# Setup of a two-layer graph-attention kernel: score matrix cut into four steps, all of Wv0 in flight at once, biases through products with ones, and two weight matrices sent by another queue

## The chip, the cores and the metric

The kernel runs on one core of a Trainium2 chip. The metric is the device time in microseconds (us), median of several executions. The engines are named as in the profile: PE is TensorE (PEld its weight loads), DVE is VectorE, ACT is ScalarE, POOL is GpSimd, SP is SyncE; a "q" behind a name is that engine's issuing of DMAs.

## The reference, cut to what matters

```python
# x: (128 graphs, 128 nodes, 512), adj: (128, 128, 128), nodemask: (128, 128), all float32
h = maximum(layernorm(x), 0)
# layer 0: attention with a sum per node, then three powers of the transition matrix
Xw = h @ Wv0 + bv0
e  = leaky_relu((Xw @ aw[:512])[:, None, :] + (Xw @ aw[512:])[:, :, None] + ab, 0.2)
T  = adj * exp(e);  T = T / (T.sum(-1, keepdims=True) + 1e-12)
H  = h @ Wk[0] + bk[0] + T @ h @ Wk[1] + bk[1] + T @ T @ h @ Wk[2] + bk[2]
x  = x + relu(H)
h  = maximum(layernorm(x), 0)
# layer 1: scores of one number per node
q, k = split(h @ Wqk);  agg = adj @ (k * mask)
w = mask * (q * agg).sum(-1) / sqrt(512)
x = x + softmax(w)[:, :, None] * (h @ Wv1)
```

The graphs are worked on two at a time, so there are 64 pairs and 64 iterations of a loop. Before the loop the kernel folds weights: Wv0 times aw (so a node's attention term is one dot product), the **score matrix** Wq Wk^T of layer 1 out of Wqk, and sums and differences of weight blocks for a seven-product (Strassen) form of the big products.

## The kernel before: the parts that matter

The setup as it was called, in program order (each engine works its own instructions in this order):

```python
load(0)                      # x and adjacency of pair 0 (SP), adjacency blocks agb (POOL)
...                          # aw copied to all 128 partitions (SP); chunks 0 and 1 of Wqk (ACT)
norm0(0)                     # loads pair 1, normalizes pair 0, sends h out and back by blocks (hd, hv)
attention_weights()          # Wv0 slice by slice in TWO buffers, DVE products with aw, spread; bv0, nm
score_sums(0)
attention(0, ...)            # pair 0's transition matrix t; also transposes agb on DVE
score_matrix()               # all four steps: transposes of Wqk chunks, products
stacked_weights()            # Wk in four blocks by SP; the three rows of bk copied to all partitions
t_transposed(0); begin(0); propagate(0); prepare0(0)
right0.update(combine(...))  # differences of the blocks of Wk
norm0(1); score_sums(1)
...
for p in range(NP + 1): ...  # the loop
```

In each iteration, scores of a pair are spread over all partitions through DRAM by GpSimd, once for layer 0 (`pz`) and once for layer 1 (`pw`):

```python
def spread_pair(col, name, by_dma):
    if by_dma:
        ...
        for j in range(G):
            nc.gpsimd.dma_start(d[j], t[j::S32])                            # pzd / pwd: 4 rows each
        dst = front.tile([P, G, N], FP, name=name, bufs=1)
        nc.gpsimd.dma_start(dst.rearrange("p g n -> p (g n)"), bcast(d, 0, G * N))   # pz / pw: 128 rows
        return dst
```

GpSimd also sends the four block loads `agb` of a pair (256 rows each), so it sends 4 x 256 + 2 x 128 + 4 x 4 = 1296 rows per iteration (a row is one contiguous piece for one partition).

## Time and profile before

| | before |
|---|---|
| median of 3 runs | 2400.05 us (2398.68 to 2400.31) |
| span of the profiled execution | 2394.7 us (its run took 2396.55) |
| TensorE busy | 2338.7 us, 98% |
| idle TensorE before the first wide run | 26.1 us of 57.67 |
| normal iteration | 35.98 us |

I cut traces at four events: the start; the first "wide run" (36 products of t and sx, the first that needs everything of the setup); the first product of layer 1 (e with x); the last aggregate product (h with aT); the end. Busy times by stretch, kernel before (columns: stretch, length, busy us of PE, weight loads, DVE, ACT, POOL with counts, granted clock, DMA share, GB/s):

```profile
0.00:57.67 57.67, 31.54 (x110) 18.96 (x110) 32.89 (x83) 19.32 (x42) 14.45 (x35) 1.00 0.86 231
57.67:100.26 42.59, 38.32 (x178) 33.13 (x178) 28.81 (x77) 7.86 (x16) 1.69 (x3) 1.00 0.32 88
100.26:2359.27 2259.01, 2252.42 (x8589) 1597.95 (x8589) 1754.84 (x4769) 605.19 (x1487) 351.89 (x605) 1.00 0.38 100
2359.27:2394.70 35.43, 16.45 (x35) 6.72 (x33) 14.07 (x33) 3.04 (x12) 1.68 (x3) 0.77 0.17 55
```

Length less PE busy is TensorE's idle time: 26.1, 4.3, 6.6 and 19.0 us. I call the third stretch "the loop" below. One caution on the clock column: it counts the trace's clock records, and time ahead of the first record appears as 1.00. Here the first record is at 33.4 us, and the weight loads just before it were spaced as at half the clock (0.82 us, then 0.43), so the 1.00 of the first stretch is no reading.

### The profile page before, as it was taken

Reading aid. Unit: us, or ns where it says so; the run is one execution under the profiler, and the core shown is the slowest. Engines: PE = TensorE matmul, PEld = TensorE weight load, DVE = VectorE, ACT = ScalarE, POOL = GpSimd, SP = SyncE. Lnnn points to the kernel's source line nnn. Section 1 sums busy time; section 2 is a strip of 40 time slices with the busy share of each in tenths; the row PEclk is TensorE's granted clock in tenths of the full one; section 3 lists DMA queues with packets and bytes.
Section 4 is the critical chain, followed back from the end, with each engine's and each line's share of the span. In section 5 each row is a group of like instructions: output and inputs, shape, how many; then the busy total and the mean of one; then the engine's idle time right before and its main releaser. Section 6 shows DMA issues by size and latency. Waiting matters only on the chain.

```text
span 2394.7 us, 27824 instructions
## 1 busy us (share of the span) xinstructions
PE 2338.7 (98%) x8909; PEld 1656.8 (69%) x8909; DVE 1830.6 (76%) x4958; ACT 635.4 (27%) x1557; POOL 369.7 (15%) x646
## 2 busy tenths in 40 slices
PE   5999999999999999999999999999999999999996
PEld 3676676776776776776776776766766766766763
DVE  5777877877877877878878878778778778778764
ACT  3222222222222222222222223223222222222221
POOL 2011111111111111111111111111111111111100
PEclk9999999999999999999999999999999999999998
DMA  8244343343343343343343343442433443443321
GB/s 227 70 112 112 82 115 102 92 114 103 92 106 105 98 106 103 100 106 100 103 106 100 103 106 86 117 106 82 121 105 81 116 110 83 115 112 82 108 67 49
DMA packets 259300, 245.62 MB, mean 103 GB/s; under 512 B 28560, under 2 KB 184336, under 8 KB 259152
## 3 DMA queue, kind: packets, MB, share of 16 engines
q1 hardware_dynamic: 232624, 216.65, 31.9%
q0 software_dynamic: 22304, 25.09, 5.9%
q10 hardware_dynamic: 4224, 2.10, 0.3%
q8 instruction: 70, 1.15, 0.2%
q14 instruction: 78, 0.64, 0.1%
HBM read 142.93 MB, written 100.79 MB: 102 GB/s over the span
## 4 chain that ended last, share of the span: by engine, by line
PE 86%; DVE 6%; DMA 4%; issue 2%; ACT 1%; POOL 0%; DVEq 0%; SPq 0%; POOLq 0%; ACTq 0%
PE pm L367 72%; PE pt L346 8%; PE pt L442 4%; DMA pwd<-pwt 2%; DMA pw<-pwd 1%; PE pt L334 1%; DVE st L224 1%; PE pm L212 1%; PE pt L330 1%; DVE x L279 1%; DVE x L407 0%; DVE sx L354 0%; DVE sx L353 0%; DVE sx L355 0%; DMA pzd<-pzt 0%
## 5 line engine op out<-in xcount | busy, mean ns | idle before, releaser
L367 PE MATMUL pm<-t,sx 128*128 128x256 f32 x2304 | 507.9, 379 | 1.9 <-DVE sx L354 1.9
L367 PEld LDWEIGHTS pm<-t,sx 128*128 128x128 f32 x2304 | 437.6, 190 | 62.1 <-DVE sx L354 2.7
L367 PE MATMUL pm<-b,x 128*128 128x256 f32 x1536 | 363.0, 379 | 0.0
L367 PE MATMUL pm<-f,sx 128*128 128x512 f32 x768 | 352.9, 595 | 4.8 <-DVE s L421 4.8
L367 PEld LDWEIGHTS pm<-b,x 128*128 128x128 f32 x1536 | 282.2, 190 | 59.6 <-issue 29.7
L290 POOL DMA_DIRECT2D pzd<-pzt x126 | 69.9, 556 | 1443.4 <-DVE pzt L287 1443.2
L367 PEld LDWEIGHTS pm<-f,sx 128*128 128x128 f32 x768 | 145.4, 191 | 191.3 <-issue 159.0
L367 PE MATMUL pm<-e,x 128*128 128x512 f32 x512 | 242.9, 597 | 13.7 <-DVE x L279 13.7
L348 ACT COPY x<-pt 128x512 f32<-128x512 f32 x256 | 147.6, 576 | 356.1 <-PE pt L346 356.1
L346 PE MATMUL pt<-tt,h 128*128 128x256 f32 x1024 | 231.5, 379 | 0.0
L262 DVE SCALAR_TENSOR_TENSOR junk<-h,u_bc 128x512 f32<-128x512 f32 x256 | 177.1, 692 | 64.3 <-ACT h L239 52.9
L346 PEld LDWEIGHTS pt<-tt,h 128*128 128x128 f32 x1024 | 194.5, 190 | 26.9 <-ACT tt L335 0.4
L367 PE MATMUL pm<-b,sx 128*128 128x256 f32 x768 | 176.2, 379 | 0.0
L367 PE MATMUL pm<-t,x 128*128 128x256 f32 x768 | 176.2, 379 | 0.0
L367 PEld LDWEIGHTS pm<-e,x 128*128 128x128 f32 x512 | 97.6, 191 | 110.6 <-issue 90.2
L279 DVE STREAM_TRANSPOSE x<-hv 128x512 f32<-128x512 f32 x256 | 166.3, 687 | 7.5 <-DMA hv<-hd 5.6
L307 ACT ACTIVATE s<-s 128x256 f32<-128x256 f32 x63 | 26.2, 416 | 522.8 <-DVE s L305 522.8
L367 PEld LDWEIGHTS pm<-t,x 128*128 128x128 f32 x768 | 145.9, 190 | 19.8
L367 PEld LDWEIGHTS pm<-b,sx 128*128 128x128 f32 x768 | 145.9, 190 | 19.8
L77 POOL DMA_DIRECT2D agb<-in_adj_dram x256 | 152.9, 602 | 18.1 <-DVE aT L319 7.4
L239 ACT ACTIVATE h<-xg,rs 128x512 f32<-128x512 f32 x128 | 97.2, 806 | 184.2 <-DVE rs L236 184.2
L442 PE MATMUL pt<-h,aT 128*128 128x512 f32 x256 | 130.6, 592 | 0.0
(119 smaller groups left out, 2792.7 us busy)
## 6 DMA issues: line engine op xcount, KB each, us to landing
hd<-h SPq DMA_DIRECT2D x128, 512.0 KB, 3.9
hv<-hd SPq DMA_DIRECT2D x512, 128.0 KB, 5.3
xg<-in_x_dram SPq DMA_DIRECT2D x64, 512.0 KB, 3.6
out_dram<-x SPq DMA_DIRECT2D x64, 512.0 KB, 2.8
ag<-in_adj_dram SPq DMA_DIRECT2D x64, 128.0 KB, 2.9
agb<-in_adj_dram POOLq DMA_DIRECT2D x256, 32.0 KB, 4.5
pz<-pzd POOLq DMA_DIRECT2D x63, 128.0 KB, 5.3
pw<-pwd POOLq DMA_DIRECT2D x63, 128.0 KB, 3.3
```

What stands on the lines that cost most here:

```text
L77: nc.gpsimd.dma_start(agb[p][c * S32:(c + 1) * S32].rearrange("p g q i -> p (g q) i"), v[c])
L212: nc.tensor.matmul(pm[c], wt[0][:, c * P:(c + 1) * P], wt[1], start=(o == 0), stop=(o == DC - 1))
L224: nc.vector.bn_stats(st, src[:, j, :])
L239: nc.scalar.activation(h[:, j, :], src[:, j, :], AF.Relu, bias=rs[:, 1, j:j + 1], scale=rs[:, 0, j:j + 1])
L262: nc.vector.scalar_tensor_tensor(junk, h[:, j, :], 1.0, u_bc[:, a, :], op0=OP.mult, op1=OP.mult, accum_out=s[:, a * G + j:a * G + j + 1])
L279: nc.vector.transpose(dst[:, j].rearrange("p f (n b) -> p f n b", n=Q), hv[:, j].rearrange("p n (f a) -> p f n a", f=Q))
L290: nc.gpsimd.dma_start(d[j], t[j::S32])
L307: nc.scalar.activation(ex, z, AF.Exp)
L346: nc.tensor.matmul(pt[:, c].rearrange("p k n -> p (k n)"), h[:, j, at:at + P], tt[:, j].rearrange("p k n -> p (k n)"), start=True, stop=True)
L348: nc.scalar.copy(X[p][:, 1:3, j, kh].rearrange("p k c n -> p c k n"), pt)
L367: nc.tensor.matmul(bank[:, :r.shape[-1]], left[i][:, k, c * P:(c + 1) * P], r, start=(first and at == 0), stop=(at == len(chunks) - 1), sk ...
L442: nc.tensor.matmul(pa, AT[p][:, j, :], H2[p][:, j, :], start=True, stop=True)
```

## The change

Its intent: start the score matrix as soon as Wqk is there, fill TensorE's waits for pair 0's attention with its four steps, remove the copies of aw, bv0 and bk to all partitions, have all of Wv0 in flight at once, and take the larger part of Wk (W1, W2) off SyncE's line. The core of the diff:

```diff
-    load(0)
+    load_x(0)                                  # agb of pairs 0 and 1 comes later
...
-    nc.sync.dma_start(aw_bc..., bcast(aw, 0, 2 * D))
+    f = [const.tile([P, HC, 2, HD], FP, name=f"f{i}") for i in range(1, 5)]   # room of later weights
+    wv0_sb = [...]                             # four slices of Wv0, aw_bc and a row of aw lie in f
+    ones = const.tile([P, P], FP, name="ones")
...
+    nc.scalar.dma_start(awr, aw.rearrange("n o -> o n"))
+    for c in range(DC):
+        nc.sync.dma_start(wv0_sb[c], wv0[c * P:(c + 1) * P])
...
+    def wv0_sums():
+        for a in range(2):
+            nc.tensor.matmul(pb, ones[0:1, :], awr[:, a * D:(a + 1) * D], start=True, stop=True)
+            nc.scalar.copy(aw_bc[:, a, :], pb)
...
-            nc.vector.scalar_tensor_tensor(junk, bv_bc, 1.0, aw_bc[:, a, :], ...)
+            nc.vector.scalar_tensor_tensor(awc[:, a], awc[:, a], 1.0, bvc, ...)   # 4 columns
+        for a in range(2):
+            nc.tensor.matmul(pc[:, 0:1], ones, ccol[:, a:a + 1], start=(a == 0), stop=(a == 1))
...
     def block0(pool, name, kh, nh):
+        if kh == nh == 0:
+            nc.gpsimd.tensor_copy(t[:, 1, 0, 0:1], wv0_sb[0][:, 0:1])   # gate: after slice 0
         for k in range(1, K):
-            nc.sync.dma_start(t[:, k], src.rearrange("(c p) o -> p c o", p=P))
+            nc.gpsimd.dma_start(t[:, k], src.rearrange("(c p) o -> p c o", p=P))
...
-        PZ[p] = spread_pair(s, "pz", p > 0)
+        PZ[p] = spread_pair(s, "pz", p > 1)    # pair 1 by TensorE
...
     norm0(0)
+    load_x(1)
+    wv0_sums()
+    ...                                        # bvc, awc, ab_bc, bsum, nm: small loads by SP
+    score_matrix(0)
+    stacked_weights()
+    score_matrix(1)
     attention_weights()
+    masks()
     score_sums(0)
+    score_matrix(2)
     attention(0, ...)
-    score_matrix()
-    stacked_weights()
+    score_matrix(3)
+    bias()
```

More of the change, by code (lines that the diff above doesn't have):

```diff
@@ L68, in load, with load_x @@
     def load(p):
+        load_x(p)
+        load_agb(p)
+    def load_x(p):
         s = slice(p * G, (p + 1) * G)
@@ L73, in load, with load_agb @@
         nc.sync.dma_start(ag[p], adj[s].rearrange("b n m -> n b m"))
+    def load_agb(p, gate=None):
+        s = slice(p * G, (p + 1) * G)
         agb[p] = loads.tile([P, G, Q, S32], FP, name="agb", bufs=2)
+        if gate is not None:
+            nc.gpsimd.tensor_copy(agb[p][:, 0, 0, 0:1], gate)
         v = adj[s].rearrange("g (q b) (c i) -> c b (g q) i", b=S32, i=S32)
@@ L86 @@
     ab_bc = setup.tile([P, 1], FP, name="ab_bc")
+    awc = setup.tile([P, 2, DC], FP, name="awc")
+    bvc = setup.tile([P, DC], FP, name="bvc")
     wpool = setup_ctx.enter_context(tc.tile_pool(name="wpool", bufs=2))
-    uctx = ExitStack()
-    upool = uctx.enter_context(tc.tile_pool(name="upool", bufs=2))
-    aw_bc = upool.tile([P, 2, D], FP, name="aw_bc", bufs=1)
-    nc.sync.dma_start(aw_bc.rearrange("p a d -> p (a d)"), bcast(aw, 0, 2 * D))
-    bv_bc = upool.tile([P, D], FP, name="bv_bc", bufs=1)
+    b12 = setup.tile([P, K, HC, HD], FP, name="b12")
+    f = [const.tile([P, HC, 2, HD], FP, name=f"f{i}") for i in range(1, 5)]
+    wv0_sb = [f[c // 2].rearrange("p c k o -> p (c k o)")[:, c % 2 * D:(c % 2 + 1) * D]
+              for c in range(DC)]
+    aw_bc = f[2].rearrange("p c k o -> p (c k o)").rearrange("p (a d) -> p a d", a=2)
+    awr = f[3].rearrange("p c k o -> p (c k o)")[0:1]
     ident = const.tile([P, P], FP, name="ident")
@@ L97 @@
     nc.vector.memset(eps, EPS)
+    ones = const.tile([P, P], FP, name="ones")
+    nc.vector.memset(ones, 1.0)
     def spread(dst, col):
@@ L107, in wqk_chunk @@
         return w
-    wchunks = {o: [wqk_chunk(a, o) for a in range(2)] for o in range(2)}
+    nc.scalar.dma_start(awr, aw.rearrange("n o -> o n"))
+    wchunks = {0: [wqk_chunk(a, 0) for a in range(2)]}
+    for c in range(DC):
+        nc.sync.dma_start(wv0_sb[c], wv0[c * P:(c + 1) * P])
+    wchunks[1] = [wqk_chunk(a, 1) for a in range(2)]
     u_bc = const.tile([P, 2, D], FP, name="u_bc")
@@ L117, with attention_weights @@
     wscale = const.tile([P, B], FP, name="wscale")
-    def attention_weights():
+    def wv0_sums():
+        for a in range(2):
+            pb = ps_t.tile([P, D], FP, name="pt")
+            nc.tensor.matmul(pb, ones[0:1, :], awr[:, a * D:(a + 1) * D], start=True, stop=True)
+            nc.scalar.copy(aw_bc[:, a, :], pb)
         for c in range(DC):
-            w = upool.tile([P, D], FP, name="wv0_sb")
-            nc.sync.dma_start(w, wv0[c * P:(c + 1) * P])
             for a in range(2):
                 junk = front.tile([P, D], FP, name="junk", bufs=1)
-                nc.vector.scalar_tensor_tensor(junk, w, 1.0, aw_bc[:, a, :], op0=OP.mult,
+                nc.vector.scalar_tensor_tensor(junk, wv0_sb[c], 1.0, aw_bc[:, a, :], op0=OP.mult,
                                                op1=OP.mult, accum_out=ucol[:, a, c:c + 1])
-        nc.sync.dma_start(bv_bc, bcast(bv0, 0, D))
-        nc.sync.dma_start(ab_bc, bcast(ab, 0, 1))
-        nc.sync.dma_start(nm, nodemask)
+    def attention_weights():
         for a in range(2):
@@ L135, in attention_weights, with masks @@
         for a in range(2):
-            junk = front.tile([P, D], FP, name="junk", bufs=1)
-            nc.vector.scalar_tensor_tensor(junk, bv_bc, 1.0, aw_bc[:, a, :],
-                                           op0=OP.mult, op1=OP.mult, accum_out=ccol[:, a:a + 1])
-        nc.vector.tensor_scalar(cz, ccol[:, 0:1], ccol[:, 1:2], ab_bc, op0=OP.add, op1=OP.add)
+            nc.vector.scalar_tensor_tensor(awc[:, a], awc[:, a], 1.0, bvc, op0=OP.mult,
+                                           op1=OP.mult, accum_out=ccol[:, a:a + 1])
+        pc = ps_t.tile([P, D], FP, name="pt")
+        for a in range(2):
+            nc.tensor.matmul(pc[:, 0:1], ones, ccol[:, a:a + 1], start=(a == 0), stop=(a == 1))
+        nc.vector.tensor_add(cz, pc[:, 0:1], ab_bc)
+    def masks():
         pm = ps_t.tile([P, DC, P], FP, name="pt")
@@ L154, in block0, with combine @@
     def block0(pool, name, kh, nh):
-        t = pool.tile([P, K, HC, HD], FP, name=name)
+        t = b12 if pool is None else pool.tile([P, K, HC, HD], FP, name=name)
         rows(t[:, 0], wk[0, :, nh * HD:(nh + 1) * HD], kh)
+        if kh == nh == 0:
+            nc.gpsimd.tensor_copy(t[:, 1, 0, 0:1], wv0_sb[0][:, 0:1])
         for k in range(1, K):
             src = wk[k, kh * HD:(kh + 1) * HD, nh * HD:(nh + 1) * HD]
-            nc.sync.dma_start(t[:, k], src.rearrange("(c p) o -> p c o", p=P))
+            nc.gpsimd.dma_start(t[:, k], src.rearrange("(c p) o -> p c o", p=P))
         return t
-    def combine(b11, b12, b21, b22, name, shape):
-        t = [const.tile([P] + shape, FP, name=f"{name}{i}") for i in range(1, 5)]
+    def combine(b11, b12, b21, b22, t):
         nc.vector.tensor_sub(t[0], b12, b11)
@@ L177, in stacked_weights, with bias @@
         blocks0["b11"] = block0(const, "b11", 0, 0)
-        blocks0["b12"] = block0(bpool, "b12", 0, 1)
+        blocks0["b12"] = block0(None, "b12", 0, 1)
         blocks0["b22"] = block0(const, "b22", 1, 1)
         blocks0["b21"] = block0(const, "b21", 1, 0)
-        nc.sync.dma_start(bsum, bcast(bk, 0, D))
-        for k in range(1, K):
-            t = bpool.tile([P, D], FP, name="bk_bc")
-            nc.sync.dma_start(t, bcast(bk, k * D, D))
-            nc.vector.tensor_add(bsum, bsum, t)
+    def bias():
+        pb = ps_t.tile([P, D], FP, name="pt")
+        nc.tensor.matmul(pb, ones[:K, :], bsum[:K], start=True, stop=True)
+        nc.scalar.copy(bsum, pb)
     e = {(kh, nh): e01 if (kh, nh) == (0, 1) else
@@ L190, with score_matrix @@
     right1 = {}
-    def score_matrix():
-        pm = [ps_m.tile([P, D], FP, name="pm") for _ in range(DC)]
-        for o in range(DC):
-            ws = wchunks.pop(o)
-            wt = []
-            for a in range(2):
-                p = ps_t.tile([P, DC, P], FP, name="pt")
-                for c in range(DC):
-                    nc.tensor.transpose(p[:, c, :], ws[a][:, c, :], ident)
-                t = wpool.tile([P, D], FP, name=f"wt{a}")
-                if a:
-                    nc.scalar.copy(t, p.rearrange("p c i -> p (c i)"))
-                else:
-                    nc.scalar.copy(t.rearrange("p (f c a) -> p f c a", f=Q, c=DC),
-                                   p.rearrange("p c (f a) -> p f c a", f=Q))
-                wt.append(t)
-            if o + 2 < DC:
-                wchunks[o + 2] = [wqk_chunk(a, o + 2) for a in range(2)]
-            for c in range(DC):
-                nc.tensor.matmul(pm[c], wt[0][:, c * P:(c + 1) * P], wt[1],
-                                 start=(o == 0), stop=(o == DC - 1))
-        for c in range(DC):
-            for nh in range(2):
-                nc.scalar.copy(e[c // HC, nh][:, c % HC, 0, :], pm[c][:, nh * HD:(nh + 1) * HD])
+    pms = []
+    def score_matrix(o):
+        if o == 0:
+            pms.extend(ps_m.tile([P, D], FP, name="pm") for _ in range(DC))
+        ws = wchunks.pop(o)
+        wt = []
+        for a in range(2):
+            p = ps_t.tile([P, DC, P], FP, name="pt")
+            for c in range(DC):
+                nc.tensor.transpose(p[:, c, :], ws[a][:, c, :], ident)
+            t = wpool.tile([P, D], FP, name=f"wt{a}")
+            if a:
+                nc.scalar.copy(t, p.rearrange("p c i -> p (c i)"))
+            else:
+                nc.scalar.copy(t.rearrange("p (f c a) -> p f c a", f=Q, c=DC),
+                               p.rearrange("p c (f a) -> p f c a", f=Q))
+            wt.append(t)
+        if o + 2 < DC:
+            wchunks[o + 2] = [wqk_chunk(a, o + 2) for a in range(2)]
+        for c in range(DC):
+            nc.tensor.matmul(pms[c], wt[0][:, c * P:(c + 1) * P], wt[1],
+                             start=(o == 0), stop=(o == DC - 1))
+            if o == DC - 1:
+                for nh in range(2):
+                    nc.scalar.copy(e[c // HC, nh][:, c % HC, 0, :], pms[c][:, nh * HD:(nh + 1) * HD])
     def norm_relu(src, name, pool):
@@ L248, in norm0 @@
     def norm0(p):
-        if p + 1 < NP and p + 1 not in xg:
+        if 0 < p < NP - 1:
             load(p + 1)
@@ L316, in attention, with transposed_adj @@
             nc.vector.tensor_scalar(t[:, j, :], ex[:, j, :], d[:, 1, j:j + 1], None, op0=OP.mult)
+        if p > 0:
+            transposed_adj(p)
+    def transposed_adj(p):
         AT[p] = front.tile([P, G, N], FP, name="aT", bufs=3)
@@ L481 @@
     norm0(0)
+    load_x(1)
+    wv0_sums()
+    nc.sync.dma_start(bvc, bv0.rearrange("(p c) -> p c", c=DC))
+    nc.sync.dma_start(awc, aw.rearrange("(a p c) o -> p a (c o)", a=2, c=DC))
+    nc.sync.dma_start(ab_bc, bcast(ab, 0, 1))
+    nc.sync.dma_start(bsum[:K], bk)
+    nc.sync.dma_start(nm, nodemask)
+    score_matrix(0)
+    stacked_weights()
+    score_matrix(1)
     attention_weights()
+    masks()
     score_sums(0)
+    score_matrix(2)
     attention(0, front.tile([P, D], FP, name="junk", bufs=1)[:, :G * N])
-    uctx.close()
-    bpool = setup_ctx.enter_context(tc.tile_pool(name="bpool", bufs=1))
-    score_matrix()
-    stacked_weights()
+    score_matrix(3)
+    bias()
     t_transposed(0)
@@ L492 @@
     prepare0(0)
-    right0.update(combine(name="t", shape=[K, HC, HD], **blocks0))
+    right0.update(combine(t=[const.tile([P, K, HC, HD], FP, name=f"t{i}") for i in range(1, 5)],
+                          **blocks0))
+    load_agb(0, X[0][:, 1, 0, 0, 0, 0:1])
+    load_agb(1)
+    transposed_adj(0)
     norm0(1)
@@ L518 @@
         if p == 0:
-            right1.update(combine(e[0, 0], e[0, 1], e[1, 0], e[1, 1], "f", [HC, 2, HD]))
+            right1.update(combine(e[0, 0], e[0, 1], e[1, 0], e[1, 1], f))
             setup_ctx.close()
```

## The prediction

> **What bounds the kernel now.** I read the page first (engine totals, slices), then the waits of TensorE in three parts of the run, then the busy times of the stretches that these marked off, then the timeline of TensorE and of the queues in the first 60 us. The totals say TensorE:
>
> ```profile
> span 2394.7 us, 27824 instructions
> PE 2338.7 (98%) x8909; PEld 1656.8 (69%) x8909; DVE 1830.6 (76%) x4958; ACT 635.4 (27%) x1557; POOL 369.7 (15%) x646
> ```
>
> Span less busy is 56 us of idle TensorE in the whole run; a change that adds idle nowhere and removes no products can't win more than that. The busy times by stretch (columns: stretch, its length, PE, weight loads, DVE, ACT, POOL, granted clock, DMA share, GB/s) say where the 56 us lie:
>
> ```profile
> 0.00:28.58 28.58, 3.99 (x10) 1.57 (x10) 14.29 (x47) 8.85 (x19) 12.70 (x32) 1.00 0.92 239
> 28.58:57.67 29.09, 27.54 (x101) 17.39 (x101) 18.60 (x36) 10.47 (x23) 1.75 (x3) 1.00 0.81 223
> 57.67:130.00 72.33, 68.06 (x279) 52.32 (x280) 50.92 (x136) 16.54 (x34) 6.90 (x12) 0.98 0.35 92
> 130.00:2320.00 2190.00, 2183.41 (x8356) 1553.48 (x8355) 1713.00 (x4664) 590.34 (x1455) 345.00 (x593) 1.00 0.38 101
> 2320.00:2394.70 74.70, 55.72 (x168) 31.99 (x166) 33.79 (x77) 9.21 (x26) 3.37 (x6) 0.89 0.17 53
> ```
>
> The idle is 24.6 us before 28.58, 1.5 to 57.67 (where the first wide run of layer 0's products with t and sx begins), 4.3 to 130, 6.6 in the whole loop, 19.0 at the end. The diff touches only the setup and the first iteration, so its room is the first 25 us, with the next 1.5. There, the timeline of TensorE (start, length, instruction, idle before it and its releaser) reads:
>
> ```profile
> 16.18 0.45 PE L101 MATMUL pt<-ident,ucol 128*128 128x128 f32 x1 [16.18 <-DVE r L231]
> 25.46 0.48 PE L101 MATMUL pt<-ident,ucol 128*128 128x128 f32 x1 [3.90 <-DVE junk L125]
> ...
> 28.58 0.47 PE L101 MATMUL pt<-ident,col 128*128 128x128 f32 x1 [1.91 <-DVE junk L262]
> 28.84 2.34 PE L201 MATMUL pt<-ident,w 128*128 128x128 f32 x10
> ```
>
> L201 is the first transpose of the score matrix (Wqk). It needs nothing but chunk 0 of Wqk, asked for at 0.8 us, yet stands behind the attention chain: Wv0 product by product, its spread, pair 0's score sums. That chain is late because Wv0 comes in two buffers:
>
> ```profile
> 6.05 0.95 SPq L122 DMA_DIRECT2D wv_sb<-in_L_gnn_Wv_dram  x2
> 16.93 0.33 SPq L122 DMA_DIRECT2D wv_sb<-in_L_gnn_Wv_dram  x1
> 20.86 0.45 SPq L122 DMA_DIRECT2D wv_sb<-in_L_gnn_Wv_dram  x1
> 24.74 0.65 DVE L125 SCALAR_TENSOR_TENSOR junk<-wv_sb,aw_bc 128x512 f32<-128x512 f32 x1
> ```
>
> The fourth slice is asked for at 20.86 and worked on at 24.74. After 28.58 TensorE is the bound: 27.5 of 29.1 us busy. DMA is full meanwhile, 92% at 239 GB/s, so bytes are the second limit of the setup.
>
> **What the Trainium skill says.** "TensorE: Matmul & The Clock Gate", Part 1, says that the array starts at half clock and reaches the full one after about 3.4 us of sustained work, and falls back when idle. The trace before agrees in size: weight loads of the score products start 0.82 us apart at 32.7 to 33.5 and 0.43 us apart from 33.5 on, about 5 us after steady work began; so pieces spread over a gappy stretch can cost double. "DMA: Bandwidth & Descriptors", section "Issuing engines are not separate DMA queues", says that transfers of all issuing engines share the same 16 DMA engines and another issuer saves only issue time. The 92% share over three queues fits. So moving W1/W2 to GpSimd's queue gives no bandwidth; what it can remove is waiting in SyncE's line. "SBUF — State Buffer", in its note on DVE blocking software DMA, warns that descriptors made by GpSimd stall while DVE runs a two-port instruction; the trace before has the small adjacency DMAs on that queue at a steady 0.58 us each beside DVE work, and the DVE work of the setup is of two-input kinds, so I count nothing for it.
>
> **The change part by part.**
> *Bytes.* Gone: the copies of aw to all partitions (0.5 MB), of bv0 (0.25) and of three bk rows (0.75): 1.5 MB, at 239 GB/s 6.3 us of DMA. The adjacency blocks for several pairs, 20 x 32 KB = 0.64 MB in the first 29 us, move behind W0: another 2.7 us. What must land before pair 0's seven products are complete: x and adjacency of pairs 0 and 1 (1.3 MB), Wqk 2.1, Wv0 1.0, h out and back 1.0, Wk 3.1: 8.5 MB, 36 us at 239 GB/s, with 1 us to start about 37; the last block (b21, 0.8 MB) is for the last product alone, so b22 lands near 33. Before, the DVE differences that wait for b22 and b21 started at 40.1 and 43.85.
>
> *Attention chain.* With aT's transpose moved out, the DVE wait of 4.3 us for the adjacency blocks before pair 0's normalization goes, and h comes at about 10 instead of 14. All Wv0 in flight from about 2 us: with x, adjacency and the first half of Wqk that is 2.7 MB, 11 us at 239 GB/s, and some of it later because W1/W2 start as soon as slice 0 is there: about 15. The eight DVE products, 0.69 + 0.08 us = 0.74 each, follow the slices and end near 18 instead of 26.1; spread and copies (2 x 0.59) 20; four score sums of 0.74, 23; pair 0's attention took 31.4 to 34.5, so it ends about 27. Some 8 us earlier. The new bias dot is on 4 columns instead of two products of 0.69: 1 us less of DVE.
>
> *TensorE.* This is the sum that decides. Until 57.67 it did 4.0 + 27.5 = 31.5 us of work; ten lone transposes of 0.45 us are nearer 0.2 when others stand behind them, which leaves about 29. Added: two products with ones for aw (each two instructions of 512 columns, cold 0.85 each: 3.4, though some of it in time that is idle anyway), one for bk (0.9), two narrow ones for cz and two spreads of pair 1 (about 1): 3.5 to 4 us that count. Chunk 0 of Wqk is there at about 8 to 9 us (in the first 29 us such a chunk took a median of 9.4 us to land, under more traffic than now). So even a TensorE that is never idle after that gets to the point of 57.67 at 8.5 + 29 + 4 = 41.5. It will be idle: steps 0 and 1 (each 0.95 transposes + 3.7 products = 4.65 us warm, about 8 cold) fill 8.5 to about 20, then it waits for the spread, for pair 0's score sums, for the copy of each transposed chunk, and for the third and fourth chunk, which are asked for only when steps 0 and 1 have freed their buffers. I take 3 us idle: 44.5. That is 13 us earlier than 57.67.
>
> *Behind it.* The same in count of instructions. Pair 1's spread by TensorE replaces a DMA round of 4 to 8 us, which before was not waited for at 61.5; it is needed because the first products now come sooner. Loads of Wv1, pair 2 and the adjacency blocks of pairs 0 and 1 fall into the first products. I give back 1 us for DVE waiting on one of them. The 3.3 us wait near 100 (its chain is pair 2's score spread through DRAM) is not touched.
>
> Sum: 2400 - 13 + 1 - 1 (less DVE work on the way, bk's additions out of the middle of pair 0's sums) = 2387.
>
> **The rivals.**
> *A: the steps fill everything and the DMA is the bound.* Then pair 0's wide products start when b22 is there and its differences (2 x 1.75 us) done, near 37, and the run is 2380. For: bytes fall, queues no longer block each other. Against: the count above needs 41.5 for TensorE alone unless the cold products with ones vanish in idle time.
> *B: the pieces stay in program order on TensorE.* Then step 2 waits for pair 0's score spread at about 24, so steps 2 and 3 end at 34, transposing t takes 1.5, propagation 3.6, DVE's sums of x 3: about 43 to 45, 2386 to 2388; with half-clock pieces 3 us more, 2391.
> *C: contention.* W1/W2 start right behind the first Wv0 slice, on a third queue; if that queue takes a third of the DMA, Wv0 and Wqk chunks 1 to 3 come 5 us later and both chains stretch: about 2393.
> *D: given back.* In-order DVE waits in the first products for pair 1's h (it goes out behind Wk) or for the late adjacency blocks: up to 5 us, 2391; more would show as idle TensorE between 45 and 60.
>
> **Range and chances.** The room (24.6 + 1.5 us idle, less the 8 us until the first chunk) caps the gain at about 18 to 22 us: below 2378 is unlikely. The low end is A with luck, the high end C and D together: 2378 to 2396. Two per cent is 48 us, more than twice the room, so faster by 2% is next to excluded; slower by 2% would need a new wait in each of 64 iterations, and the diff leaves the loop as it was.
>
> **What would show it.** Right: score transposes start before 10 us; the four Wv0 loads stand together at about 2 us; pair 0's wide run with sx starts at 40 to 47 instead of 57.67; idle TensorE before it about 12 us instead of 26; the loop from there on as long as before to within 3 us. Wrong: TensorE idle for over 4 us between steps 1 and 3; a Wv0 slice landing after 18; DVE waiting for pair 1's h or adjacency between 40 and 60; idle in the loop above 6.6 us, which would mean that the order of the instructions moved there as well.

## The result, and the profile after

| | before | after |
|---|---|---|
| median (6 runs each) | 2400.09 us | 2384.62 us (2381.57 to 2387.23) |
| span of the profiled execution | 2394.7 | 2381.4 |

The ratio is 0.9937, with a 95% interval of 0.9924 to 0.9949. Ratios here are the mean time of one kernel's runs over that of the other's of the same rounds, so not quite the ratio of the medians. The result lies in the range and 2.4 us from the predicted value. But the sum that gave that value was not right in its parts.

The totals and the same four stretches of the changed kernel:

```profile
span 2381.4 us, 27851 instructions
PE 2343.4 (98%) x8921; PEld 1660.8 (70%) x8921; DVE 1828.5 (77%) x4956; ACT 637.7 (27%) x1560; POOL 374.3 (16%) x653
```

```profile
0.00:48.13 48.13, 37.72 (x121) 21.94 (x122) 28.98 (x78) 18.67 (x39) 11.62 (x30) 0.93 0.83 246
48.13:91.49 43.36, 38.55 (x178) 33.05 (x178) 30.23 (x80) 9.83 (x22) 9.07 (x16) 1.00 0.29 81
91.49:2343.88 2252.39, 2249.70 (x8589) 1598.72 (x8589) 1755.25 (x4769) 606.16 (x1487) 351.93 (x605) 1.00 0.38 101
2343.88:2381.40 37.52, 17.45 (x35) 7.05 (x33) 14.07 (x33) 3.04 (x12) 1.68 (x3) 0.75 0.16 51
```

| stretch | before | after | difference |
|---|---|---|---|
| to the first wide run | 57.67 | 48.13 | -9.5 |
| to the first product of layer 1 | 42.59 | 43.36 | +0.8 |
| the loop | 2259.01 | 2252.39 | -6.6 |
| the tail | 35.43 | 37.52 | +2.1 |
| span | 2394.7 | 2381.4 | -13.3 |

These are one execution of each kernel; by the medians the gain is 15.5 us, 2.2 more than the table splits up. So half of the table's gain stands where no line of the diff is: the loop has the same 8589 products before and after, and is 6.6 us shorter; its idle TensorE fell from 6.6 to 2.7 us. And the setup gave 8.8 us rather than 12.

**The setup after.** TensorE's timeline (start, length, line, operation, idle before it and its releaser):

```profile
6.10 1.11 PE L231 MATMUL pt<-ident,w 128*128 128x128 f32 x4
8.85 3.13 PE L231 MATMUL pt<-ident,w 128*128 128x128 f32 x12 [1.63 <-DMA w<-in_L_gnn_Wqk_dram]
11.77 4.83 PE L242 MATMUL pm<-wt,wt 128*128 128x512 f32 x8
17.61 3.70 PE L242 MATMUL pm<-wt,wt 128*128 128x512 f32 x8 [1.01 <-ACT wt L234]
...
27.34 0.47 PE L117 MATMUL pt<-ident,col 128*128 128x128 f32 x1 [2.86 <-DVE junk L292]
...
35.86 3.70 PE L242 MATMUL pm<-wt,wt 128*128 128x512 f32 x8
...
48.13 8.04 PE L402 MATMUL pm<-t,sx 128*128 128x256 f32 x36 [0.72 <-DVE sx L389]
```

The score matrix's transposes now start at 6.10 us, wait once for chunk 0's second half until 8.85, and steps 0 and 1 run early, as intended. But pair 0's score spread (L117 on `col`) is at 27.34, only 1.2 us earlier than the 28.58 of before. DVE shows why:

```profile
7.77 0.69 DVE L148 SCALAR_TENSOR_TENSOR junk<-f,f 128x512 f32<-128x512 f32 x1
...
13.16 1.29 DVE L254 BATCH_NORM_STATS2 st<-xg 128x6 f32<-128x512 f32 x2 [4.69 <-DMA xg<-in_x_dram]
...
19.04 0.17 DVE L159 SCALAR_TENSOR_TENSOR awc<-awc,bvc 128x4 f32<-128x4 f32 x1 [3.99 <-DMA awc<-in_L_gnn_aw_dram]
...
22.89 0.69 DVE L148 SCALAR_TENSOR_TENSOR junk<-f,f 128x512 f32<-128x512 f32 x1
...
33.50 0.48 DVE L346 TENSOR_SCALAR t<-junk,d 128x128 f32<-128x128 f32 x2
```

Between the Wv0 products (L148) DVE has, in its order, the statistics of pair 1's x and the small product for the bias. It stood 4.69 us for x of pair 1 and 3.99 us for a transfer of 4 KB. Wv0 itself had landed before (its four loads were asked for by 3.7 us and took 5.5 us in the median). The last Wv0 product ended at 23.6 instead of the predicted 18, and pair 0's t at 34.0 (before: 34.5) instead of 27. Who was in the way shows in what GpSimd and ScalarE issued:

```profile
6.61 5.93 POOL L190 DMA_DIRECT2D b<-in_L_gnn_Wk_dram  x8
```

```profile
10.68 5.76 ACTq L122 DMA_DIRECT2D w<-in_L_gnn_Wqk_dram  x2
```

The eight loads of W1/W2 (2 MB) went out from 6.6 us on, as soon as Wv0's first slice was there. The small loads behind them took about 10 us to land, and ScalarE stood 5.8 us issuing two loads of Wqk (2.1 us in e8) while finished transposes waited for its copies (the 1.01 at 17.61). Between 10 and 20 us the DMA engines moved 369 GB/s, so it was not that little was moved, but that the wrong bytes came first. The Trainium skill, "DMA: Bandwidth & Descriptors", section "Queues, rings and completion order", says that each DMA engine takes turns between the queue rows that have work; this fits with a third queue taking its share at once, and the 10 us here against 4.0 to 5.2 us in experiment e8 for the same loads is the size of it. The other wait, for pair 1's x, is not explained so: SyncE asked for this x only at 6.46 us, after standing 2.7 us for a load of Wv0, and in e8, with W1/W2 out of the way, DVE still stood 4.36 us for it.

**The clock.** TensorE did 37.72 us of work up to the first wide run. Of these, 4.80 lie ahead of 8.85 us, about where my sum of 33 us begins; 32.9 lie behind it. The stretch's granted clock was 0.93 (with the first clock record at 14.2 us, so not to be compared with the 1.00 of before). By tens of us:

```profile
10.00:20.00 10.00, 8.95 (x22) 4.69 (x23) 2.84 (x13) 1.91 (x4) 2.54 (x4) 1.00 1.07 369
20.00:30.00 10.00, 5.91 (x30) 4.36 (x29) 7.50 (x27) 4.48 (x10) 0.00 (x0) 0.72 0.92 211
30.00:40.00 10.00, 10.00 (x29) 4.91 (x28) 9.01 (x23) 4.66 (x13) 0.00 (x0) 0.93 0.68 207
```

TensorE's gaps in 20 to 30 us (5.9 of 10 busy) go with a clock of 0.72 there; in e8, where the same ten us are 9.3 busy, the trace has no drop. The clock record of the drop is 6.827 us long (24.5 to 31.3) at 0.5, twice 3.413 us, and one at 92.8 us is 3.413 long. The Trainium skill, "TensorE: Matmul & The Clock Gate", Part 1, gives 3413 ns for such a window, so here page and trace agree to the digit.

**The loop.** What shortened it is found in GpSimd's line. Before, in one iteration (711 us) and in the one ahead of it (673 us), the issue of `pw`, with the time that GpSimd stood before it:

```profile
673.15 0.59 POOL L292 DMA_DIRECT2D pw<-pwd  x1 [5.36 <-DMA pwd<-pwt]
711.38 0.59 POOL L292 DMA_DIRECT2D pw<-pwd  x1 [7.60 <-issue]
```

7.60 instead of 5.36, and released by "issue": for about 2 us GpSimd waited for nothing that the profile shows. This pause returns every ten iterations (349, 711, 1072, 1434, 1796, 2157 us). What it does, on DVE and then on TensorE:

```profile
714.97 0.42 DVE L461 TENSOR_REDUCE s<-pw 128x2 f32<-128x256 f32 x1 [1.93 <-DMA pw<-pwd]
```

```profile
729.47 1.98 PE L367 MATMUL pm<-f,sx 128*128 128x512 f32 x4 [0.66 <-DVE s L421]
```

DVE stands 1.93 us for pw, does everything behind it later, and 15 us on TensorE waits for a sum of DVE's. After the change the pause is still there, but it falls somewhere else in the iteration, ahead of a load of adjacency that is not needed for long:

```profile
655.50 0.58 POOL L87 DMA_DIRECT2D agb<-in_adj_dram  x1 [2.20 <-issue]
```

It returns at 1016, 1377, 1738 and 2098 us, always ahead of an agb load. At this point it is a correlation. The experiments e10 and e11 test it.

### The profile page after: what moved, and what is told of

Read it like the earlier page. It is cut to its first block, busy times and chain, and to the rows that moved or that the text cites.

```text
span 2381.4 us, 27851 instructions
## 1 busy us (share of the span) xinstructions
PE 2343.4 (98%) x8921; PEld 1660.8 (70%) x8921; DVE 1828.5 (77%) x4956; ACT 637.7 (27%) x1560; POOL 374.3 (16%) x653
## 4 chain that ended last, share of the span: by engine, by line
PE 90%; DVE 3%; DMA 2%; issue 1%; ACT 0%; POOL 0%; DVEq 0%; POOLq 0%; ACTq 0%
PE pm L402 75%; PE pt L381 8%; PE pt L477 4%; PE pt L369 1%; DMA pwd<-pwt 1%; PE pt L365 1%; DMA pw<-pwd 1%; DVE st L254 0%; DMA pz<-pzd 0%; DVE junk L292 0%; DMA pzd<-pzt 0%; DVE x L309 0%; DVE x L442 0%; DVE x L508 0%; DVE sx L390 0%
## 5 line engine op out<-in xcount | busy, mean ns | idle before, releaser
L402 PE MATMUL pm<-e,x 128*128 128x512 f32 x512 | 243.2, 597 | 13.5 <-DVE x L309 13.5
```

Source lines behind the costliest of these rows:

```text
L402: nc.tensor.matmul(bank[:, :r.shape[-1]], left[i][:, k, c * P:(c + 1) * P], r, start=(first and at == 0), stop=(at == len(chunks) - 1), sk ...
```

## The experiments

They came in three calls of four, each with its own runs of the kernel before on the same chip (medians 2399.31, 2396.05 and 2397.68 us). All gave correct outputs. The theories, as they grew:

1. The front's gain needs the interleaved steps and the earlier data together (e1, e2).
2. W1/W2 start too early; held back, the front is shorter (e3, e8; e12 by another queue).
3. The loop's gain comes of where GpSimd's pause falls (e4, e6, e7 tried to shift it with memsets; e10, e11 with rows). Rival: of something in the front or in the addresses.
4. Addresses modulo 256 bytes matter (formed after e4; e6, e7, e9).

### e1: the four steps alone

```diff
-    def score_matrix():
+    def score_matrix(steps):        # as before, for the given steps
...
     norm0(0)
+    score_matrix((0, 1))
     attention_weights()
     score_sums(0)
+    score_matrix((2,))
     attention(0, ...)
     uctx.close()
     bpool = ...
-    score_matrix()
+    score_matrix((3,))
```

> The kernel before with one part of the change alone: the score matrix in four steps, two of them ahead of pair 0's attention weights, one ahead of its attention, one behind. Wv0 still in two buffers, broadcasts still by DMA, W0 to W2 still on SyncE's queue. Theory 1 (the gain before the first products is TensorE's idle time filled with these steps; nothing else of the change moves the end of pair 0's attention, which stood at 34.5 us before and 34.0 after): the first wide run of products with t and sx starts at 46 to 50 us instead of 57.7, and the run takes 2390 to 2393 us, the loop being as slow as before. Rival (the bytes saved and Wv0 loaded at once are what makes the steps fit): it starts at 53 or later, 2396 or more.

Measured: 2403.43 us, ratio 1.0021 (1.0009 to 1.0033). The first wide run came at 53.94 instead of 57.67, the first product of layer 1 at 100.19 (before 100.26). The steps alone gain nothing: theory 1's numbers (46 to 50, 2390 to 2393 us) failed, the rival's (53 or later, 2396 or more) held. One line of DVE and one of TensorE:

```profile
27.54 1.30 DVE L282 STREAM_TRANSPOSE x<-hv 128x512 f32<-128x512 f32 x2 [5.90 <-DMA hv<-hd]
```

```profile
81.60 10.98 PE L370 MATMUL pm<-t,sx 128*128 128x256 f32 x36 [3.72 <-DVE sx L357]
```

My reading (the wait is measured, its cause argued): starting the steps early frees Wqk's buffers early, so chunks 2 and 3 are asked for among the loads that pair 0's attention needs. DVE stood 5.9 us for hv, and t came at 38.4 instead of 34.5. Then the clock fell, with records at 0.5 at 53.5 and 80.8 us: the 36 products that take 8.04 us at full clock took 9.46 at 53.94 and 10.98 at 81.60.

### e2: everything but the interleaving

```diff
-    score_matrix(0)
     stacked_weights()
-    score_matrix(1)
     ...
-    score_matrix(2)
     attention(0, ...)
-    score_matrix(3)
+    for o in range(DC):
+        score_matrix(o)
     bias()
```

> The changed kernel with all four steps of the score matrix put back behind pair 0's attention; all else as changed. Theory 1: the wide run starts at 54 us or later instead of 48.1, the run takes 2390 to 2394 us. Rival (earlier Wv0 and fewer bytes carry the gain): it stays within 2 us of 48.1 and the run within 2 us of the changed kernel's 2385.

Measured: 2386.83 us, ratio 0.9952 (0.9939 to 0.9965).

```profile
54.92 8.04 PE L402 MATMUL pm<-t,sx 128*128 128x256 f32 x36 [0.72 <-DVE sx L389]
```

First wide run at 54.92 (2.75 earlier than before), first product of layer 1 at 97.15 (3.1 earlier). With e1's 3.7 and 0.1, the two halves add up to 6.5 and 3.2, but together they gave 9.5 and 8.8: they need each other. Measured from this side (e2 against after), the interleaving is worth 6.8 us at the wide run and 5.7 us at layer 1. And e2 has the loop of the changed kernel, 2252.0 us, without the interleaving; so the loop's gain does not come of the steps. That is also why the run missed theory 1's 2390 to 2394 us, though the wide run met its 54. In whole runs the interleaving is worth less surely than in the front: the intervals of e2's ratio and of the change's (0.9924 to 0.9949) overlap.

### e3: the gate later, but only for one block

```diff
-            nc.gpsimd.tensor_copy(t[:, 1, 0, 0:1], wv0_sb[0][:, 0:1])
+            nc.gpsimd.tensor_copy(t[:, 1, 0, 0:1], ucol[:, 1, DC - 1:DC])
```

> The changed kernel with the transfers of W1 and W2 on GpSimd's queue held until the last Wv0 product, not the first Wv0 slice. The order of instructions on TensorE and VectorE is the same. Theory 2 (they start at 6.6 us and hold up pair 1's x and the small bias columns, for which in-order VectorE waited 4.7 and 4.0 us between Wv0 products, so that the attention chain won only 0.5 us): the last Wv0 product ends at 15 to 19 us instead of 23.5, the wide run starts at 44 to 46.5 instead of 48.1, the run takes 2 to 4 us less than the changed kernel. Rival (W1 and W2 are needed that early): the differences of W wait for them, the wide run starts at 48 or later, and the run is as long or longer.

Measured: 2383.98 us, ratio 0.9938; first wide run 50.05, later than after's 48.13. The experiment missed its aim, and the trace shows how:

```profile
1.64 5.21 POOL L190 DMA_DIRECT2D b<-in_L_gnn_Wk_dram  x7
```

```profile
17.69 1.29 DVE L254 BATCH_NORM_STATS2 st<-xg 128x6 f32<-128x512 f32 x2 [9.31 <-DMA xg<-in_x_dram]
```

The gate writes only b11's W1, so only that one load waits for it. The other seven, which the old gate had held up too, because it stood ahead of them in line, went out at 1.64 us, ahead of nearly everything. DVE then stood 9.31 us for pair 1's x. A failed experiment, but one that shows contention from the other side: with most of W1/W2 five us earlier the front was 1.9 us longer.

### e4, e6, e7: memsets on GpSimd, to shift its pause

```diff
+    scr = const.tile([P, 12], FP, name="scr")     # e4 on before: 12; e6 on before: 5; e7 on after: 9
     for t in cols:
         nc.gpsimd.memset(t, 0.0)
+    for i in range(12):
+        nc.gpsimd.memset(scr[:, i:i + 1], 0.0)
```

> The kernel before with twelve one-column memsets added on GpSimd in the setup, nothing else. Theory 3 (the 6.6 us that the changed kernel won inside the loop, which the diff leaves alone, come from where in an iteration GpSimd's stream of instructions pauses, every tenth iteration: before it pauses just ahead of the DMA that spreads the layer 1 scores, and VectorE and then TensorE wait; the changed kernel has more GpSimd instructions ahead of the loop, and its pause falls on a load that nobody waits for): setup as before (wide run at 57 to 59 us), the pause falls on another DMA, the iterations of 37 us that came every tenth are gone, 2394 to 2397 us. Rival (the loop gained because it starts in another order or at another time): 2399 to 2401 as before.

> The kernel before with five memsets on GpSimd in the setup instead of twelve. Twelve had left GpSimd's pause on the DMA that spreads the layer 1 scores, because some twelve to thirteen instructions make one iteration, yet the kernel got 9.6 us faster. Theory 3 as corrected (the phase of GpSimd's stream decides the loop): with five the pause falls ahead of an adjacency load as in the changed kernel, the excess of the long iterations behind the third falls from 10.4 us to 3 to 6, and the run takes 2392 to 2396 us. Rival (any extra instruction early on GpSimd shifts the start of the DMAs, and what twelve won was won there, not by the phase): long iterations every tenth as before, whatever the total.

> The changed kernel with nine memsets on GpSimd in the setup, so that by the count the pause goes back from the adjacency load to the DMA that spreads the layer 1 scores. Theory 3: long iterations every tenth as in the kernel before, excess behind the third 8 to 12 us instead of 4.9, the run 3 to 6 us slower than the unaltered changed kernel of this call; the setup as it was. Rival (the loop's gain has another cause): within 2 us of it.

And the changed kernel once more:

> The changed kernel unaltered, for a second trace and for times on the chip of the next three. Expected 2382 to 2387 us; first wide run of products with t and sx within 1.5 us of 48.1; iterations that last over 36.2 us about as few as in its first trace (six behind the third), GpSimd's pause of 2.2 us again ahead of an adjacency load.

Measured: e4 2388.31 us (ratio 0.9960), e6 2403.78 (1.0031), e5 2382.42 (0.9942), e7 2377.62 (0.9921). In none of them did the pause move: it stayed ahead of pw in e4 and e6 and ahead of agb in e7. So the pause doesn't count instructions, the numbers that theory 3 had given for e4, e6 and e7 all failed (e5's expectation held), and the times moved for another reason. All engines' orders were the same as in the kernel they were made from; what differed was the memsets and the little tile. The tile shifts every buffer that is allocated behind it, so which buffer counts is not separated here. The starts of the buffers of loads (x, adjacency), of hv, of x1, pz and pw, modulo 256 bytes, as compiled, and the median landing of the 128 KB pieces of hv in the loop:

| kernel | start mod 256 | hv lands in | run |
|---|---|---|---|
| before | 192 | 5.3 us | 2396 to 2400 |
| e4 (on before) | 0 | 4.9 | 2388.31 |
| e6 (on before) | 224 | 6.3 | 2403.78 |
| e5 (after) | 192 | 5.2 | 2382.42 |
| e7 (on after) | 0 | 4.6 | 2377.62 |

The DMA view's lines (transfer, queue, count, size, median us to landing) for before, e6 and e7:

```profile
hv<-hd SPq DMA_DIRECT2D x472, 128.0 KB, 5.3
```

```profile
hv<-hd SPq DMA_DIRECT2D x472, 128.0 KB, 6.3
```

```profile
hv<-hd SPq DMA_DIRECT2D x480, 128.0 KB, 4.6
```

The Trainium skill, "DMA: Bandwidth & Descriptors", section "How a descriptor splits into AXI transactions", says that a piece of a transfer that doesn't start at a multiple of 256 bytes fetches from the multiple below, and that the unused bytes cost too. The page words this for bytes that are read; hv is written into these buffers, so it is no more than a hint here. The order agrees where the starts are 0 against the others. That 224 is a whole us worse than 192 I can't derive from it; for that the measurement stands alone. Before and after have the same 192, so this is not part of what the change did; it is a gain that lay beside it. e9 tests the alignment again, with tiles that VectorE writes, so that GpSimd's memsets stay out of it.

### e8: all of W1/W2 held back

```diff
-        if kh == nh == 0:
-            nc.gpsimd.tensor_copy(t[:, 1, 0, 0:1], wv0_sb[0][:, 0:1])
+        nc.gpsimd.tensor_copy(t[:, 1:3, 0, 0], ucol[:, 1, DC - 2:DC])   # each block, after the last Wv0 product
...
-    for t in cols:
-        nc.gpsimd.memset(t, 0.0)
+    for i, t in enumerate(cols):
+        (nc.vector if i > 2 else nc.gpsimd).memset(t, 0.0)              # keeps GpSimd's count
```

> The changed kernel with all eight transfers of W1 and W2 held until the last Wv0 product (the earlier attempt held one, and the other seven went out at 1.6 us instead of 6.6; wide run 1.9 us later). Three of GpSimd's six first memsets go to VectorE so that the number of its instructions, and the phase of its pause, stay. Theory 2 (contention of W1/W2 with pair 1's x, the bias columns and Wqk stretches both chains): pair 1's x lands by 12 us, the last Wv0 product ends at 16 to 19 instead of 23.5, the wide run starts at 40 to 45 instead of 48.1, the run takes 3 to 7 us less than the unaltered changed kernel. Rival (they are needed early): the differences of W wait for them and the wide run starts at 48 or later.

Measured: 2377.05 us, ratio 0.9920; beside e5 5.4 us less. The wide run, DVE's wait for pair 1's x, and its t:

```profile
42.25 8.04 PE L401 MATMUL pm<-t,sx 128*128 128x256 f32 x36 [0.72 <-DVE sx L388]
```

```profile
12.71 1.29 DVE L253 BATCH_NORM_STATS2 st<-xg 128x6 f32<-128x512 f32 x2 [4.36 <-DMA xg<-in_x_dram]
...
28.85 0.48 DVE L345 TENSOR_SCALAR t<-junk,d 128x128 f32<-128x128 f32 x2
```

The loads went out at 19.6 instead of 6.6 us. DVE no longer waited for the 4 KB transfer. For pair 1's x it waited nearly as long as in after (4.36 and 4.69 us; x came at 12.7, not by 12 as expected), so this wait is not W1/W2's doing. The last Wv0 product ended at 19.0 instead of 23.6, t was ready at 29.3 instead of 34.0, and the wide run began 5.9 us earlier than in after. No clock record of this stretch is below 1.0, and TensorE's work in it was 35.66 us instead of 37.72 on the same 121 products: 2.1 us of after's work were clock. It beats both kernels.

### e9: e8 with aligned buffers

```diff
+    pad = const.tile([P, 16], FP, name="pad")
+    nc.vector.memset(pad, 0.0)
...
+    spad = small.tile([P, 8], FP, name="spad", bufs=1)
+    nc.vector.memset(spad, 0.0)
```

> The candidate to beat all: the kernel of e8_gate_all (W1/W2 held back until the last product of Wv0) with two tiles of padding, 64 bytes in the constant pool and 32 in the small one, so that the buffers of the loads, of the front and of the late pool start at multiples of 256 bytes instead of 192 or 160 past one; every engine's order but for two memsets as in e8. Theory of alignment (e4 -11 us against before, e7 -4.8 us against e5, both at starts 0 modulo 256): 2369 to 2374 us, loop 2246 to 2249 us instead of 2251.0, hv landing in 4.5 to 4.9 us instead of 5.2, the vector engine's wait for pw in the loop under 4 us. Rival (e7's gain came of something else that its tile moved, such as the buffers of the strip steps): 2375 to 2379 us and hv at 5.2.

Measured: 2372.00 us (2371.73 to 2372.78), ratio 0.9895 (0.9881 to 0.9908). Loop 2248.1 us, hv in 4.6 us, DVE's wait for pw in the loop 2.5 us in all. Each of the expected numbers of the theory held and the rival's did not. (Its wide run came at 43.63, 1.4 us later than e8's.) This is the best version: 25.7 us below the kernel before.

### e10 and e11: the pause moved by rows

e10, on the kernel before (addresses and order of compute untouched):

```diff
-        nc.sync.dma_start(ag[p], adj[s].rearrange("b n m -> n b m"))
+        (nc.gpsimd if 2 <= p < 4 else nc.sync).dma_start(ag[p], adj[s].rearrange("b n m -> n b m"))
```

> The kernel before with one thing moved: the loads of ag of pairs 2 and 3 (2 x 256 rows, two issues) are sent by GpSimd instead of SyncE; all addresses and the order of all compute as before. If GpSimd's pause of some 2 us comes after a count of rows sent (an iteration sends 1296), it comes 512 rows = 0.4 iteration earlier: ahead of an agb load near 697 us (and near 1058, 1781, 2142) instead of ahead of pw<-pwd at 711. Theory that the pause on pw makes the loop's long iterations: excess after iteration 3 falls from 10.4 to 3 to 6 us, loop 2259 to 2252-2255, run 2391 to 2396 beside a before of 2396 to 2400. Rival (the pause's place costs nothing, the loop's gain in the change comes of something else): pause moved but loop within 2 us of 2259 and the run as before. If the pause stays at 711, rows are not what is counted.

e11, on the changed kernel: the same line with `2 <= p < 6`.

> The changed kernel with the loads of ag of pairs 2 to 5 (4 x 256 rows, four issues) sent by GpSimd instead of SyncE; addresses and the order of compute as in after, the front of the first 90 us untouched. By the count of rows the pause comes 1024 rows earlier, which is 272 rows later of an iteration: from ahead of the fourth agb load to ahead of pw<-pwd or just behind it. Theory of the pause's place: if it falls on pw, long iterations come back every tenth, loop 2251-2252 to 2255-2259, run 2384 to 2390. Rival: loop within 2 us of 2252 wherever the pause falls, run 2380 to 2384.

Measured: e10 2391.42 us (2389.95 to 2394.59), ratio 0.9977, loop 2252.4 us. e11 2392.70 us (2387.01 to 2394.06), ratio 0.9976, loop 2262.9 us. The pause in e10, and two of e11's:

```profile
698.66 0.58 POOL L77 DMA_DIRECT2D agb<-in_adj_dram  x1 [2.23 <-issue]
```

```profile
266.99 0.59 POOL L322 DMA_DIRECT2D pw<-pwd  x1 [7.40 <-issue]
...
1356.05 0.58 POOL L322 DMA_DIRECT2D pw<-pwd  x1 [9.32 <-ACT tt L370]
```

In e10 it was expected at 697, 1058, 1781 and 2142 us and came at 698.66, 1059.02, 1782.27 and 2142.51, each ahead of an agb load. Two loads moved in the second and third iteration made the loop of the kernel before 6.6 us shorter, to the 2252.4 of the changed kernel; excess over the normal iteration behind iteration 3 fell from 10.4 to 4.1 us. In e11 the pause went back to pw (267 and 2080 us by itself, and in the iterations between at 630, 993, 1356 and 1719 as waits of 8 to 9 us before pw), long iterations returned every tenth, and all of the loop's gain was lost and 4 us more than it. The run came out 2.7 us above the top of what I had expected, the loop 3.9 us: the theory had the direction and was short in size. DVE's wait for pw in the loop (150 to 2290 us; total, times, longest), in before, after, e10 and e11:

```profile
DVE s L461 <- DMA pw<-pwd: 24.0, 29, 2.7
```

```profile
DVE s L496 <- DMA pw<-pwd: 12.2, 21, 2.2
```

```profile
DVE s L461 <- DMA pw<-pwd: 13.8, 20, 2.9
```

```profile
DVE s L496 <- DMA pw<-pwd: 26.5, 24, 3.1
```

Some 10 us of DVE's waits go with the pause in e10, and 14 us come with it in e11. All kernels together (each loop is that of one profiled execution):

| buffers start at | pause ahead of pw: loop, us | pause ahead of agb: loop, us |
|---|---|---|
| 224 | e6 2268.2 | |
| 192 | before 2259.0, e1 2263.7, e11 2262.9 | after 2252.4, e5 2251.3, e2 2252.0, e3 2250.5, e8 2251.0, e10 2252.4, e12 2249.8 |
| 0 | e4 2253.2 | e7 2247.4, e9 2248.1 |

Within the row of 192, the two columns don't overlap (means 2261.9 and 2251.3). That both causes act on the same spot, a later pw costing less when transfers land faster, fits DVE's waits for pw (24.0 us in before and 13.5 in e4; 12.2 in after and 1.7 in e7), but was not tested by itself.

### e12: W1/W2 on SyncE's queue

```diff
-        if kh == nh == 0:
-            nc.gpsimd.tensor_copy(t[:, 1, 0, 0:1], wv0_sb[0][:, 0:1])
         for k in range(1, K):
-            nc.gpsimd.dma_start(t[:, k], ...)
+            nc.sync.dma_start(t[:, k], ...)
```

> The changed kernel with the eight loads of W1/W2 on SyncE's queue at the same place of the program, and no gate copy: what the part with GpSimd's queue is worth by itself. They would be asked for at some 9 to 14 us behind Wv0 and the small loads and hold back what SyncE sends next. Theory of contention: what counts is only when they begin, so the first wide run is within 46 to 51 us as in after (48) and the run 2380 to 2388. Rival that SyncE's queue as such held the front (pair 0's hd and hv wait behind eight sends of 1.2 us): wide run 51 to 56, run 2385 to 2393. GpSimd sends 2048 rows fewer, so its pause falls elsewhere too and the loop may differ by up to 7 us.

Measured: 2378.14 us, ratio 0.9920.

```profile
42.80 5.45 PE L400 MATMUL pm<-t,sx 128*128 128x256 f32 x24 [1.46 <-DVE sx L387]
```

The first wide run came at 42.80, earlier than either side had expected, and the run was below both ranges: in SyncE's line the loads stand behind the small ones and are spread over 18 to 30 us, so they start late by themselves, as in e8. Not all of it stays: TensorE then waited once 6.1 us for x of layer 1, and the first product of layer 1 came at 88.51 (after 91.49, e8 85.98). The part of the change that moved W1/W2 to GpSimd's queue thus made the kernel slower, by 4 to 5 us (e5, the same kernel with them on GpSimd's queue, had 2382.42 us; the ratios to before are 0.9942 and 0.9920, and their intervals, 0.9930 to 0.9955 and 0.9907 to 0.9934, just overlap). Its gate was set too early, not its queue wrong: gated late, the same queue gives e8.

## Why the prediction was right or wrong

The value and the chances held, and that is luck: the time up to layer 1 fell 3.2 us less than foreseen and the tail lost 2.1 us unforeseen, while the loop won 6.6 us unforeseen.

- **Room and bound: right.** What bounds the setup is TensorE behind pair 0's attention chain, and the gain stayed under the room of 18 to 22 us.
- **Attention chain, "8 us earlier": wrong**, 0.5 us. The step that failed is the one that let DVE's products follow the slices of Wv0 and end near 18. The slices were there; DVE's order puts the statistics of pair 1's x and the bias product between them, and those waited 4.7 and 4.0 us. The second wait is rival C's contention, in another place than I had put it: not Wv0 came late, but the small loads, which W1/W2 had overtaken. e8 shows it by taking W1/W2 away: that wait goes, t is 4.7 us earlier, the wide run 5.9. The first wait stays in e8 (4.36 us). I had left it out altogether: pair 1's x, asked for at 6.46 us, stands in DVE's line among the Wv0 products.
- **TensorE's sum, wide run at 44.5: mis-sized**, 48.1, outside the 40 to 47 that I had given as a sign of being right. The sum was 8.5 + 33 + 3 (chunk 0, work, idle). Cut at the same place it was 8.85 + 32.9 + 6.4. So the term that failed is the 3 us of idle: TensorE idled 4.1 us between steps 1 and 3 alone, one of my signs of being wrong. The work came out at its value, but 2.1 us of it are clock (after beside e8), so without these it would have been about 2 us less than I had reckoned.
- **Given back behind it, 1 us: right**, 0.8.
- **"The loop from there on as long as before to within 3 us": wrong**, it lost 6.6 us. I reasoned that the diff leaves the loop as it was. Its instructions it does, but W1/W2 on GpSimd's queue and pair 1's spread by TensorE change how many rows GpSimd has sent by then (8 x 256 more and 136 fewer), and a pause that comes with what it has sent moved off pw. (In e12, with W1/W2 on SyncE's queue, it is ahead of an agb load too, so W1/W2's part in the move was not needed.) e10 puts the same gain into the kernel before, e11 takes it away from the changed one. The change got it by accident.
- **The tail** lost 2.1 us, which the prediction didn't have. The trace has 1.0 of it in a longer wait of TensorE for the last pair's layer 1 (10.45 and 11.45 us) and 1.0 more of busy time on the same 35 products at a clock of 0.75 instead of 0.77. No experiment was made on it; tails of all runs lie between 35.4 and 37.9 us without following a part of the change.
- **Rivals A, B and D**: A fell (DMA moved 300 GB/s in the first 27 us, so the 239 that I had reckoned with was no limit; and e8, with the same loads in another order, reaches the wide run 5.9 us earlier, so their amount was not the bound). Of B the order of steps came true, with step 3 at 35.9 to 39.6 instead of 34, and its range, 2386 to 2391, is off by the loop. D was 0.8 us.

What stays open: what the pause is. It lasts about 2 us, doesn't follow GpSimd's instructions, and moves when GpSimd sends more transfers. I count the transfers in all fourteen traces: everywhere the pause settles to exactly 100 of them, or 12,960 rows, which is ten iterations (in e12 after a distance of 102 and one of 101). Extra loads of 256 rows move it as rows do: at the first pause GpSimd had sent 14,336 to 14,464 rows in before and 14,328 to 14,584 in e10, 14,688 to 14,944 in after and 14,680 to 14,808 in e11. But before and after don't agree with each other, so rows alone are not what is counted.

## What to carry to other kernels

A transfer that is let go "as soon as possible" is not free: hold large loads that are needed late back behind the small ones that an in-order engine is waiting for, and look at that engine's own order, not only at the buffers, to see which load it will stand for. When a change gains or loses in a stretch that it doesn't touch, look for something periodic whose phase it moved and for addresses that it shifted, and test each by moving it alone; a control as small as a 48-byte tile with its twelve memsets moved this kernel by 11 us. A prediction that lands on the number is to be checked part by part like one that misses.

## What the Trainium skill lacked or had wrong

- "DMA: Bandwidth & Descriptors" has no pause in the issuing of DMAs by GpSimd. Here it stands 1.7 to 2.4 us without a visible cause every ten iterations (about 361 us, 12,960 rows sent), and its place is worth 6.6 us (e10) to 10.5 us (e11) of the loop.
- The same page's section on how a descriptor splits gives extra transactions for starts that aren't multiples of 256 bytes, but no time. It speaks of bytes read, not of writes. Here transfers of 128 KB into SBUF landed in 4.6 to 4.9 us at 0, 5.2 to 5.7 at 192 (ten traces) and 6.3 at 224 modulo 256; the shift as a whole was worth 4.8 us (e7 beside e5) and 11.0 us (e4 beside before), and cost 7.7 us (e6 beside before).
- The same page's section "Issuing engines are not separate DMA queues" holds here, but doesn't warn that a further queue can cost something: 2 MB let go early on a third queue (6.6 us) made loads of 2 to 4 KB land in 9.8 to 10.1 us, against 4.2 to 5.2 with the same queue held until 19.6 us (after beside e8).
